# One semaphore per gather buffer, one-hots for two groups at a time, and one more hand-filled group each for ScalarE and VectorE, in a graph network layer

## The chip, the cores and the metric

One Trainium2 chip, one core. The metric is the device time of one execution in microseconds. The engines named below are PE (TensorE, matrix products; its weight loads are counted apart as PEld), DVE (VectorE), ACT (ScalarE), POOL (GpSimd, which here issues the indirect DMAs) and SP (SyncE, which issues the other DMAs). Each engine works through its own list of instructions in the order in which the program gives them, and engines wait for each other through semaphores.

## The reference

One message-passing layer over a graph of 12,500 nodes with 128 features and 400,000 edges, all in float32. The edges are sorted by their target node. Cut to what matters:

```python
h = jnp.maximum(_layernorm(x, axis=-1), 0.0)
e = jnp.concatenate([h[src], h[dst], edge_attr_32], axis=-1)      # 400000 x 288
m = jax.nn.relu(e @ w1 + b1) @ w2 + b2
agg = jax.ops.segment_sum(m, dst, num_segments=12500)
gi, gh = agg @ w_ih + b_ih, h @ w_hh + b_hh                       # GRU gates r, z, n
x + (1 - z) * n + z * h
```

## The kernel before

**Tiling.** 128 edges are a tile; 8 tiles are a group. The 3,125 tiles make 391 groups, numbered k from 0, of which the first has 5 tiles. A group is worked on in two halves, called units: unit u = 2k + h.

**What a group needs.** The product `e @ w1` is split in three. The part of the source node, `A = h @ w1[0:128]`, is computed once for all nodes in a first phase and written to DRAM. The part of the target node, `B`, too; since edges are sorted, a half group touches a window of at most 32 nodes, so its rows of B come as a block into `RW`, and a transposed one-hot `L` (made on DVE at L575) times `RW` adds them on PE into the PSUM tile `pre` (L673, which also does the edge attributes). The source rows are at random places, and there are four ways to get them:

- *Gathered*: POOL issues eight indirect DMAs (L156), one for each tile, that bring 128 rows of A into one of 11 buffers `G`. DVE then adds `pre` and `G` and takes the relu in one custom instruction (L701), which writes `RB`.
- *By hand on ACT*: ACT copies for each of the 1,024 edges one column of 4 bytes from `hT_all`, the transposed h that stays on the chip, into `HE_act` (L960). PE multiplies that with `w1a` into `pre` (L684), and ACT takes the relu (L710).
- *By hand on DVE*: the same with 512 instructions that pack two columns each into `both` (L967), and 8 copies that unpack them into `HE_dve` (L972).
- *By hand on SP*: 1,024 small DMAs from A into a buffer of their own.

For the addresses an engine that works by hand loads indices into its registers first: DVE 32 at a time (L945, 32 loads to a group), ACT 16 at a time.

The first 9 groups (`RAW`) gather rows of x instead of A, and are normalised on the way. `SPREAD` at L56 says how many of the other groups go by hand: 28 on ACT, 27 on DVE, 2 on SP, spread evenly over the list. That leaves 334 groups to POOL, 325 of them from A.

**Sum over edges.** A one-hot `OH` (128 edges by 32 nodes of the window for each tile, made on DVE at L623) is the weight of a product with `RB` on PE (L724), which collects two groups in one of two PSUM banks `seg`. The comparison row 0 to 31 of the one-hot stands in the unused part of the other bank. `take` copies the sums out (L733); every 14 groups a block of nodes goes through the gates (`node`).

**What sets the order.** The order of each engine's list is written out by hand (`manual_schedule`). The loop over units calls, for unit u: `gathers(u)`, then `stages(u)` with the transposed one-hot or the one-hot of group u//2 + 3, `pre(u+3)`, `add(u+2)` and `relu(u+2)`, then `seg(u)`; between them `run_jobs` puts the steps of the hand-filled groups in four portions. Each engine that fills by hand works on one group at a time, and its steps are spread over the units from the end of its last group to just before the group is needed. A gather may be put in the list once the DVE add that reads its buffer's old content stands before it.

**Semaphores.** The framework gives each indirect DMA one of eight semaphores (`DMASW0` to `DMASW7`) in turn. A DMA waits until the one eight before it, which used the same semaphore, has landed. The add of a group waits for all eight and for PE. An instruction has room for few waits; the others stand before it as EVENT_SEMAPHORE instructions of their own.

Of the kernel before, what the change touches and what calls it, by code (L numbers as in the profile page):

```python
# [9 lines left out]
F32 = mybir.dt.float32  # L10
# [19 lines left out]
V = 32  # L30
# [14 lines left out]
RAW = 9  # L45
GBUFS = 11
# [6 lines left out]
PIECE = 128  # L53
STEP = {"act": 4, "dve": 8, "sp": 4}
ROW = 4 * D
SPREAD = {"dve": 27, "act": 28, "sp": 2}  # L56
START = {"dve": 14, "act": 4, "sp": 24}
NR = 12672

# [4 lines left out]
def tile_gnn(ctx: ExitStack, tc: tile.TileContext, x, src, srcT, dstT, dstP, eaT, eaP, w1, b1, w2T, b2,  # L64
             wih, bih, whh, bhh, out):
    nc = tc.nc
    ctx.enter_context(tc.manual_schedule())
    const = ctx.enter_context(tc.tile_pool(name="const", bufs=1))
# [12 lines left out]
    def tiles(k):  # L81
        return (0 if k == 0 else SUP0 + (k - 1) * PAIR, SUP0 + k * PAIR)


    def unit_tiles(u):
        k, h = divmod(u, 2)
        t0, t1 = tiles(k)
        return [(t0 + a * GRP + j, j, a) for j in (2 * h, 2 * h + 1) for a in range(2)
                if t0 + a * GRP + j < t1]

    mode, order = {}, {m: [] for m in SPREAD}
    for m, n in SPREAD.items():
        lo, hi = START[m] // 2 + 2, NP - {"dve": 7, "act": 5, "sp": 12}[m]
        for i in range(n):
            k = lo + int((i + 1) * (hi - lo) / n)
# [46 lines left out]
    taker, ring = {}, []  # L142
    for k in range(NP):
        if k not in mode:
            taker[k] = ring[-GBUFS] if len(ring) >= GBUFS else -1
            ring.append(k)

    def gather(k):
        if k >= NP or k in mode:
            return  # L150
        G[k] = gp.tile([128, GRP, 2, D], F32, name="G")
        table = x if k < RAW else A
        for u in (2 * k, 2 * k + 1):
            for t, j, a in unit_tiles(u):
                c, i = divmod(t, CH)
                nc.gpsimd.indirect_dma_start(  # L156
                    out=G[k][:, j, a, :], out_offset=None, in_=table,
                    in_offset=bass.IndirectOffsetOnAxis(ap=src_i[c][:, i:i + 1], axis=0))

    for k in range(RAW):  # L160
        gather(k)
# [2 lines left out]
    RB = [const.tile([128, PAIR, D + 4], F32, name=f"RB{i}") for i in range(2)]  # L164
    for r in RB:
        nc.vector.memset(r[:, :, D:], 1.0)
    OHB = [const.tile([128, GRP, 2, V], F32, name=f"OH{i}") for i in range(6)]
    nc.vector.memset(OHB[0], 0.0)


# [93 lines left out]
    dloc = const.tile([128, T], F16, name="dloc")  # L264
# [78 lines left out]
    with tc.tile_pool(name="pp", bufs=3) as pp:  # L343
# [50 lines left out]
        row = lambda v: v.rearrange("(o f) -> o f", o=1)  # L394
# [34 lines left out]
        for q in range(NC + 3):  # L429
            if q < NC:  # L430
                b, i0, c, e, P, n0 = chunk(q)
# [3 lines left out]
            if 1 <= q <= NC:  # L435
                b, i0, c, e, P, n0 = chunk(q - 1)
# [6 lines left out]
            if q >= 3:  # L443
                b, i0, c, e, P, n0 = chunk(q - 3)
# [3 lines left out]
            if q < NC:  # L448
                b, i0, c, e, P, n0 = chunk(q)
# [4 lines left out]
            if 1 <= q <= NC:  # L454
                b, i0, c, e, P, n0 = chunk(q - 1)
# [12 lines left out]
            if q >= 3:  # L468
                b, i0, c, e, P, n0 = chunk(q - 3)
                if e == bats[b][1]:  # L470
                    nc.sync.dma_start(nodes(A, i0, e, P), asb[b][:P, :e, :])
            if 2 <= q <= NC + 1:
                b, i0, c, e, P, n0 = chunk(q - 2)
# [79 lines left out]
    Ls, OH, RT, HE, SEG = ({} for _ in range(5))  # L553
# [50 lines left out]
                                  "(p f) -> p f", p=V))  # L604

    def onehot(k):
        if k >= NP:
            return
        t0, t1 = tiles(k)
        OH[k] = OHB[k % len(OHB)]  # L610
        row = SEGB[((k - 3) // 2 + 1) % 2][:, 256:256 + V]
        for a in range(2) if k == 0 else (None,):
            if a is None:
                o, s = OH[k].rearrange("p j a v -> p a j v"), slice(t0, t1)
                d = dloc[:, s].rearrange("p (a j) -> p a j", a=2)[:, :, :, None]
                shape = [128, 2, GRP, V]
                i = row[:, None, None, :]
            else:
                e = min(t1, (a + 1) * GRP)
                o, d = OH[k][:, :e - a * GRP, a, :], dloc[:, a * GRP:e, None]  # L620
                shape = [128, e - a * GRP, V]
                i = row[:, None, :]
            nc.vector.tensor_tensor(o, d.to_broadcast(shape), i.to_broadcast(shape),  # L623
                                    op=ALU.is_equal)

    def unit(u):
        k, h = divmod(u, 2)
# [59 lines left out]
    def add(u):  # L687
        if u >= NU or u < 0:
            return
        k, h = divmod(u, 2)  # L690
        if h == 0 and k < NP - 1:
            return
        c = slice(0, PAIR) if k < NP - 1 else slice(GRP * h, GRP * h + GRP)
        o, p = RB[k % 2][:, c, :D], PP[k][:, c, :]
        if u in HE or k in hand:
            RT[u] = o, p
            HE.pop(u, None)
            HE.pop(u - 1, None)
            hand.pop(k, None)
        else:  # L700
            nc.vector._custom_dve(TENSOR_ADD_SAT, out=o, in0=p,  # L701
                                  in1=G[k].rearrange("p j a f -> p (j a) f")[:, c, :], s0=float("inf"), s1=0.0)
        if h == 1:
            PP.pop(k)
            G.pop(k, None)
# [9 lines left out]
    def seg(u):  # L715
        k, h = divmod(u, 2)
        p = SEGB[(k // 2) % 2]
        if h == 0 and k % 2 == 0:
            nc.tensor.matmul(p[:, :D + 1], zrow[:, :128], zrow[:, :D + 1], start=True, stop=False)  # L719
        l = unit_tiles(u)  # L720
        rest = l if h else l + unit_tiles(u + 1)
        for i, (t, j, a) in enumerate(l):
            r0 = 2 * V * (k % 2) + V * a
            nc.tensor.matmul(p[r0:r0 + V, :D + 1], OH[k][:, j, a, :],  # L724
                             RB[k % 2][:, 2 * j + a, :D + 1], start=False,
                             stop=all(b != a for _, _, b in rest[i + 1:]))

# [276 lines left out]
    def gathers(u):  # L1004
        while asked[0] < NP and (asked[0] in mode or 2 * taker[asked[0]] + 1 < u + 2):
            gather(asked[0])
            asked[0] += 1
# [13 lines left out]
    def stages(u):  # L1021
        if u + 7 >= 0:
            raw_stats(u + 7)
        if u + 6 >= 0:
            raw_fin(u + 6)
            raw_h(u + 6)
        if u % 2 == 0:
            onehot_T(u // 2 + 3)
        elif u > -7:
            onehot(u // 2 + 3)  # L1030
        if u + 4 >= 0:
            raw_turn(u + 4)
        if u + 3 >= 0:
            pre(u + 3)
        if u + 2 >= 0:
            add(u + 2)
            relu(u + 2)
# [18 lines left out]
    for u in range(NU):  # L1056
        k, h = divmod(u, 2)
# [33 lines left out]
        other(1)  # L1091
        other(2)
        seg(u)
        if u == 0:
            node_setup()
# [106 lines left out]
    f = nc.values_load(flag[0:1, 0:1], min_val=0, max_val=1)  # L1202
# [67 lines left out]
```

## Time and profile before

| what | value |
|---|---|
| time, median of 3 runs | 3404.46 us (3404.36 to 3407.26) |
| the profiled execution's own time | 3403.76 us |
| its span, first to last instruction | 3401.8 us |
| instructions | 88,642 |
| granted TensorE clock, mean | 0.796 |
| DMA | 335.44 MB, mean 99 GB/s |

The span is what the profile shows; 1.96 us of the profiled execution lie around it. Busy time counts an engine's own work; loads of registers, semaphore waits and branches are not in it, so an engine can be fully taken up with less than 100% busy. In a list of groups the last column gives the idle time just before the instructions and what ended it; "issue" means that the engine waited for nothing that the profile shows.

### The profile page before, as it was taken

To read this page: it belongs to the slowest core of one execution; us is meant where nothing else is said; L and a number is where in the kernel's file an instruction comes from. 1 tells how busy PE (TensorE), PEld (TensorE's weight loads), DVE (VectorE), ACT (ScalarE), POOL (GpSimd) and SP (SyncE) were. 2 spreads that over 40 slices of the span, in tenths; PEclk is the share of its full clock that TensorE was granted. 3 is DMA by queue.
4 is the path that set the end of the run, shared out by engine and by line. 5 is a ranking of instruction groups with operands and counts; after the bars stand their busy time and mean duration, and the time that the engine had idled before them with its cause. 6 is when DMAs were issued, how large, how long until landed. Compare 5 with 4: busy or idle time off the path is not lost. (4 is left out here: it accounts for less than half of the span.)

```text
span 3401.8 us, 88642 instructions
## 1 busy us (share of the span) xinstructions
PE 2417.4 (71%) x13113; PEld 1563.7 (46%) x13113; DVE 2225.1 (65%) x16468; ACT 3079.4 (91%) x29057; POOL 2566.1 (75%) x2678
## 2 busy tenths in 40 slices
PE   7567777777677767776777667676677767766767
PEld 7444444444445444544444444444444434444445
DVE  8556666666676666666666666666666666666665
ACT  7699999999999998999899988988988898898984
POOL 7777777777777777777777777777777777777776
PEclk9777887887887778777877877788777778777878
DMA  6434444434443333343434433443433334343332
GB/s 213 106 88 93 97 100 99 101 94 100 102 98 94 98 99 95 95 101 97 98 93 99 98 94 93 96 96 93 98 93 92 95 94 99 92 97 96 92 92 73
DMA packets 191316, 335.44 MB, mean 99 GB/s; under 512 B 66753, under 2 KB 112384, under 8 KB 190729
## 3 DMA queue, kind: packets, MB, share of 16 engines
q0 software_dynamic: 85408, 175.09, 23.0%
q1 hardware_dynamic: 105177, 154.58, 16.4%
q14 instruction: 478, 3.92, 0.4%
q8 instruction: 109, 1.79, 0.2%
q10 hardware_dynamic: 144, 0.07, 0.0%
HBM read 309.24 MB, written 20.24 MB: 97 GB/s over the span
## 5 line engine op out<-in xcount | busy, mean ns | idle before, releaser
L156 POOL DMA_INDIRECT G<-A,src_i x2600 | 2498.9, 961 | 796.2 <-issue 753.7
L960 ACT COPY HE_act<-hT_all 128x4 uint8 x28672 | 2886.8, 189 | 51.4 <-issue 27.0
L967 DVE SCALAR_TENSOR_TENSOR both<-hT_all 128x4 uint16 x13824 | 1173.4, 153 | 988.5 <-issue 980.7
L673 PE MATMUL pre<-RW,L 128*128 128x256 f32 x3128 | 1132.4, 488 | 229.8 <-DVE RB L701 220.6
L673 PEld LDWEIGHTS pre<-RW,L 128*128 128x128 f32 x3128 | 660.6, 236 | 506.1 <-DVE RB L701 234.0
L724 PE MATMUL seg<-RB,OH 128*32 128x129 f32 x6250 | 603.9, 324 | 380.0 <-DVE RB L701 349.7
L724 PEld LDWEIGHTS seg<-RB,OH 128*32 128x32 f32 x6250 | 333.1, 125 | 820.4 <-DVE RB L701 532.7
L701 DVE CUSTOM_DVE_ANT_0 RB<-pre,G 128x1024 f32<-128x1024 f32 (+1 forms) x326 | 394.5, 1210 | 62.7 <-DMA G<-A,src_i 49.2
L575 DVE TENSOR_SCALAR L<-L,node_of 64x512 f32<-64x512 int32 x382 | 186.7, 489 | 9.7 <-DMA L<-in_dstP 9.4
L719 PE MATMUL seg<-zrow 1*128 1x129 bf16 x196 | 45.3, 231 | 164.4 <-DVE OH L623 164.2
L623 DVE TENSOR_TENSOR OH<-dloc,seg 128x256 f32<-128x256 f16 (+1 forms) x392 | 159.5, 407 | 0.5 <-issue 0.5
L750 PE MATMUL nd<-spot,sums 128*128 128x40 f32 x782 | 116.6, 321 | 1.2 <-DVE sums L733 1.2
L750 PEld LDWEIGHTS nd<-spot,sums 128*128 128x128 f32 x782 | 112.4, 231 | 10.5 <-issue 9.0
L710 ACT ACTIVATE RB<-pre 128x1024 f32<-128x1024 f32 x64 | 65.0, 1015 | 52.4 <-PE pre L684 52.4
L809 ACT ACTIVATE gt<-nd 128x512 f32<-128x512 f32 (+2 forms) x28 | 16.4, 585 | 96.5 <-PE nd L803 96.5
L972 DVE COPY HE_dve<-both 128x512 uint8<-128x512 uint8 x216 | 96.6, 447 | 7.4
L684 PEld LDWEIGHTS pre<-w1a,HE_act 128*128 128x128 f32 x448 | 88.4, 245 | 11.6
L684 PEld LDWEIGHTS pre<-w1a,HE_dve 128*128 128x128 f32 x432 | 87.9, 252 | 12.1
L684 PE MATMUL pre<-w1a,HE_act 128*128 128x128 f32 x448 | 86.4, 327 | 0.0
L684 PE MATMUL pre<-w1a,HE_dve 128*128 128x128 f32 x432 | 85.1, 333 | 0.0
L156 POOL DMA_INDIRECT G<-in_x,src_i x69 | 65.9, 954 | 21.8 <-issue 20.7
L233 PE MATMUL nd<-w1b,hT_all 128*128 128x128 f32 x224 | 45.5, 346 | 43.3 <-DVE xb L835 43.3
(177 smaller groups left out, 1383.9 us busy)
## 6 DMA issues: line engine op xcount, KB each, us to landing
L<-in_dstP SPq DMA_DIRECT2D x195, 256.0 KB
L<-in_eaP SPq DMA_DIRECT2D x195, 256.0 KB
G<-A,src_i POOLq DMA_INDIRECT x2600
G_sp<-A SPq DMA_DIRECT2D x2048, 0.5 KB
RW<-B SPq DMA_DIRECT2D x782, 16.0 KB
xb<-in_x SPq DMA_DIRECT2D x26, 256.0 KB
out<-xb SPq DMA_DIRECT2D x26, 256.0 KB
xs<-in_x SPq DMA_DIRECT2D x11, 512.0 KB
```

The lines of the kernel that those rows point to most:

```text
L156: nc.gpsimd.indirect_dma_start(out=G[k][:, j, a, :], out_offset=None, in_=table, in_offset=bass.IndirectOffsetOnAxis(ap=src_i[c][:, i:i + ...
L575: nc.vector.tensor_scalar(o, i, node_of[:, k:k + 1], None, op0=ALU.is_equal)
L623: nc.vector.tensor_tensor(o, d.to_broadcast(shape), i.to_broadcast(shape), op=ALU.is_equal)
L673: nc.tensor.matmul(p[:, 2 * i:2 * i + 2, :], Ls[k // QP][:, c0:c0 + 128], RW[k % 4], start=True, stop=not raw)
L684: nc.tensor.matmul(p[:, 2 * i + a, :], cols, w1a, start=False, stop=n + 1 == len(l) or l[n + 1][1] != j)
L701: nc.vector._custom_dve(TENSOR_ADD_SAT, out=o, in0=p, in1=G[k].rearrange("p j a f -> p (j a) f")[:, c, :], s0=float("inf"), s1=0.0)
L710: nc.scalar.activation(o, p, AF.Relu)
L724: nc.tensor.matmul(p[r0:r0 + V, :D + 1], OH[k][:, j, a, :], RB[k % 2][:, 2 * j + a, :D + 1], start=False, stop=all(b != a for _, _, b in r ...
L750: nc.tensor.matmul(p[:, bass.ds(offs[i], V + SHIFT)], sums[:, slot(b, i), :D], spot[:, i % 2, :], start=False, stop=i == len(offs) - 1)
L960: nc.scalar.copy(he[:, e * 4:e * 4 + 4], column(v))
L967: nc.vector.scalar_tensor_tensor(both[:, (e0 % PIECE + i) // 2, :], column(vals[i + 1]), 256.0, column(vals[i]), op0=ALU.mult, op1=ALU.add)
L972: nc.vector.tensor_copy(he[:, p0 * 4:(p0 + PIECE) * 4].rearrange("p (n c b) -> p n c b", c=2, b=4), both.bitcast(U8).rearrange("p n (b c) ...
```

## The change

Three edits.

1. Each of the 11 buffers gets a semaphore of its own, `filled0` to `filled10`. The eight gathers of a group from A count it up by 16 each, and no longer use the framework's semaphores. Before the add DVE waits for this one semaphore to reach 128 times the number of uses of the buffer. The nine raw groups and the last group stay as they were.
2. The one-hots of two neighbouring groups are made by one instruction of twice the size. The six buffers of one group become three of two groups.
3. `SPREAD` goes to 29 groups on ACT and 28 on DVE. POOL keeps 332 groups, 323 of them from A.

```diff
-SPREAD = {"dve": 27, "act": 28, "sp": 2}
+SPREAD = {"dve": 28, "act": 29, "sp": 2}
...
+    filled = [tc.alloc_semaphore(f"filled{i}") for i in range(GBUFS)]
+    uses, goal = [0] * GBUFS, {}
+
     def gather(k):
         if k >= NP or k in mode:
             return
+        i = ring.index(k) % GBUFS
+        if RAW <= k < NP - 1:
+            uses[i] += 1
+            goal[k] = filled[i], 16 * PAIR * uses[i]
         G[k] = gp.tile([128, GRP, 2, D], F32, name="G")
...
-                nc.gpsimd.indirect_dma_start(
+                fetched = nc.gpsimd.indirect_dma_start(
                     out=G[k][:, j, a, :], out_offset=None, in_=table,
                     in_offset=bass.IndirectOffsetOnAxis(ap=src_i[c][:, i:i + 1], axis=0))
+                if k in goal:
+                    fetched.then_inc(goal[k][0], 16)
+                    tc.no_tile_sem_insts.add(fetched.ins.name)
+                    tc.add_to_no_dep_group(f"rows{k}", fetched.ins)
...
-    OHB = [const.tile([128, GRP, 2, V], F32, name=f"OH{i}") for i in range(6)]
+    OHB = [const.tile([128, 2 * PAIR, V], F32, name=f"OH{i}") for i in range(3)]
...
     def onehot(k):
-        if k >= NP:
+        if k >= NP or (k % 2 and k > 1):
             return
...
+        n = 2 if 1 < k < NP - 1 else 1
+        for i in range(n):
+            OH[k + i] = o[:, PAIR * ((k + i) % 2):PAIR * ((k + i) % 2) + PAIR, :]
+        t0, t1 = tiles(k)[0], tiles(k + n - 1)[1]
...
+        for p, e0, e1 in parts:
+            shape = [128, e1 - e0, V]
+            nc.vector.tensor_tensor(p, dloc[:, e0:e1, None].to_broadcast(shape),
+                                    row[:, None, :].to_broadcast(shape), op=ALU.is_equal)
...
         else:
-            nc.vector._custom_dve(TENSOR_ADD_SAT, out=o, in0=p,
+            if k in goal:
+                nc.vector.wait_ge(*goal[k])
+            made = nc.vector._custom_dve(TENSOR_ADD_SAT, out=o, in0=p,
                                   in1=G[k].rearrange("p j a f -> p (j a) f")[:, c, :], s0=float("inf"), s1=0.0)
+            if k in goal:
+                tc.declare_no_dep(made.ins, group=f"rows{k}", reason="behind the wait for the landing")
+                tc.declare_fence(made.ins, group=f"rows{k}")
...
-            nc.tensor.matmul(p[r0:r0 + V, :D + 1], OH[k][:, j, a, :],
+            nc.tensor.matmul(p[r0:r0 + V, :D + 1], OH[k][:, a * GRP + j, :],
                              RB[k % 2][:, 2 * j + a, :D + 1], start=False,
```

In the order of DVE's list, first two neighbouring groups before, from the one-hot ahead of the add of group 83 to the add of group 84. The ISA rows are the adds, `both` and `HE_dve` belong to a group that DVE fills by hand at that time, TENSOR_LOAD loads 32 indices, and the names in brackets are the semaphores that the instruction, or the EVENT_SEMAPHORE instructions just ahead of it, wait for:

```order
L623 TENSOR_TENSOR OH1_184<-dloc_227,seg0_79 128x2x4x32
L701 ISA RB1_180<-pre_39161,G_33482 128x8x128 [waits DMASW4_49,DMASW3_49,DMASW5_49,DMASW2_49,DMASW6_49,DMASW1_49,DMASW7_49,DMASW0_49,PE_49]
L967 SCALAR_TENSOR_TENSOR both_39049<-hT_all_60 128x4 x12
L972 COPY HE_dve_36483<-both_39049 128x512 [waits DVE_49]
L945 TENSOR_LOAD at_90
L967 SCALAR_TENSOR_TENSOR both_39877<-hT_all_60 128x4 x8
L575 TENSOR_SCALAR L_38458<-L_38458,node_of_230 64x512 [waits DMAHW4_49,DMAHW0_49]
L967 SCALAR_TENSOR_TENSOR both_39877<-hT_all_60 128x4 x8
L945 TENSOR_LOAD at_90
L967 SCALAR_TENSOR_TENSOR both_39877<-hT_all_60 128x4 x8
L623 TENSOR_TENSOR OH2_185<-dloc_227,seg0_79 128x2x4x32
L701 ISA RB0_179<-pre_39673,G_34018 128x8x128 [waits DMASW4_49,DMASW3_49,DMASW5_49,DMASW2_49,DMASW6_49,DMASW1_49,DMASW7_49,DMASW0_49,PE_49]
```

Each group has a one-hot of 256 elements in a row, and each add waits for nine semaphores. The same place in the changed kernel, from the add of group 93 to the add of group 94 (the lines have moved: 713 is the add, 633 the one-hot, 982, 987 and 960 the work by hand):

```order
L713 ISA RB1_180<-pre_45224,G_39434 128x8x128 [waits filled4,PE_49]
L960 TENSOR_LOAD at_90
L982 SCALAR_TENSOR_TENSOR both_45401<-hT_all_60 128x4 x16
L960 TENSOR_LOAD at_90
L982 SCALAR_TENSOR_TENSOR both_45401<-hT_all_60 128x4 x4
L586 TENSOR_SCALAR L_44384<-L_44384,node_of_227 64x512 [waits DMAHW4_49,DMAHW3_49]
L982 SCALAR_TENSOR_TENSOR both_45401<-hT_all_60 128x4 x12
L987 COPY HE_dve_42923<-both_45401 128x512 [waits DVE_49]
L960 TENSOR_LOAD at_90
L982 SCALAR_TENSOR_TENSOR both_46184<-hT_all_60 128x4 x8
L633 TENSOR_TENSOR OH0_183<-dloc_224,seg1_80 128x512
L713 ISA RB0_179<-pre_45680,G_39939 128x8x128 [waits filled5,PE_49]
```

Every second group makes the one-hots of two, and an add waits for two semaphores. DVE's list goes from 1,644 EVENT_SEMAPHORE instructions to 625, from 392 one-hots to 198, and gets one more group of 512 packing instructions, 32 register loads and 8 copies.

On POOL the gathers of group 42 before, and the first of the next group:

```order
L156 DMA G_14063<-A_97,src_i_1592 128x128 [waits DMASW5_49,DVE_49]
L156 DMA G_14063<-A_97,src_i_1592 128x128 [waits DMASW6_49]
L156 DMA G_14063<-A_97,src_i_1592 128x128 [waits DMASW7_49]
L156 DMA G_14063<-A_97,src_i_1592 128x128 [waits DMASW0_49]
L156 DMA G_14063<-A_97,src_i_1592 128x128 [waits DMASW1_49]
L156 DMA G_14063<-A_97,src_i_1592 128x128 [waits DMASW2_49]
L156 DMA G_14063<-A_97,src_i_1592 128x128 [waits DMASW3_49]
L156 DMA G_14063<-A_97,src_i_1592 128x128 [waits DMASW4_49]
L156 DMA G_14527<-A_97,src_i_1592 128x128 [waits DMASW5_49,DVE_49]
```

And those of group 42 in the changed kernel, with its neighbours on both sides:

```order
L163 DMA G_13796<-A_97,src_i_1590 128x128 [waits DVE_49]
L163 DMA G_13796<-A_97,src_i_1590 128x128 x7
L163 DMA G_14470<-A_97,src_i_1590 128x128 [waits DVE_49]
L163 DMA G_14470<-A_97,src_i_1590 128x128 x7
L163 DMA G_15456<-A_97,src_i_1590 128x128 [waits DVE_49]
L163 DMA G_15456<-A_97,src_i_1590 128x128 x7
```

What is left is one wait to a group, for the add that frees the buffer; the waits for the DMA eight places earlier are gone.

More of the change, by code (lines that the diff above doesn't have):

```diff
@@ L606, in onehot @@
     def onehot(k):
-        if k >= NP:
+        if k >= NP or (k % 2 and k > 1):
             return
-        t0, t1 = tiles(k)
-        OH[k] = OHB[k % len(OHB)]
+        o = OHB[(k // 2) % len(OHB)]
         row = SEGB[((k - 3) // 2 + 1) % 2][:, 256:256 + V]
[L612 to L624, printed above, removed]
+        n = 2 if 1 < k < NP - 1 else 1
+        for i in range(n):
+            OH[k + i] = o[:, PAIR * ((k + i) % 2):PAIR * ((k + i) % 2) + PAIR, :]
+        t0, t1 = tiles(k)[0], tiles(k + n - 1)[1]
+        if k:
+            parts = ((o[:, PAIR * (k % 2):PAIR * (k % 2) + t1 - t0, :], t0, t1),)
+        else:
+            parts = tuple((OH[0][:, a * GRP:min(t1, (a + 1) * GRP), :], a * GRP, min(t1, (a + 1) * GRP))
+                          for a in range(2))
+        for p, e0, e1 in parts:
+            shape = [128, e1 - e0, V]
+            nc.vector.tensor_tensor(p, dloc[:, e0:e1, None].to_broadcast(shape),
+                                    row[:, None, :].to_broadcast(shape), op=ALU.is_equal)
     def unit(u):
```

## The prediction

> **What bounds the kernel now.** I read the page's groups first, then the counts by stage of the instructions that touch `G`, then DVE's groups in the stretch from 400 to 1500 us. The page:
>
> ```profile
> PE 2417.4 (71%) x13113; PEld 1563.7 (46%) x13113; DVE 2225.1 (65%) x16468; ACT 3079.4 (91%) x29057; POOL 2566.1 (75%) x2678
> L156 POOL DMA_INDIRECT G<-A,src_i x2600 | 2498.9, 961 | 796.2 <-issue 753.7
> L960 ACT COPY HE_act<-hT_all 128x4 uint8 x28672 | 2886.8, 189 | 51.4 <-issue 27.0
> L967 DVE SCALAR_TENSOR_TENSOR both<-hT_all 128x4 uint16 x13824 | 1173.4, 153 | 988.5 <-issue 980.7
> ```
>
> By busy share ACT would be the bound. But POOL's idle time is all "issue": 753.7 us between 2,600 gathers, 0.3 us ahead of each. Busy and idle together are 2498.9 + 796.2 = 3295 us, the whole run but its first 92 us. The line's own view and two pieces of POOL's timeline show that it never stops:
>
> ```profile
> L156 POOL DMA_INDIRECT G<-A,src_i x2600: 940/945/1552, 92.3 to 3383.9; - x186
> 5.92 0.94 POOL L156 DMA_INDIRECT G<-in_x,src_i  x1 [0.30 <-issue]
> 203.40 0.95 POOL L156 DMA_INDIRECT G<-A,src_i  x1 [0.72 <-DVE RB L701]
> ```
>
> From the first to the last start are (3383.9 - 92.3) / 2599 = 1.2665 us a gather. The gather at 5.92 us, the third of the run, has no wait for an earlier DMA and still a gap of 0.30 us, so the gap is not a wait for semaphores.
>
> Does POOL set the end, or does it only happen to be busy until then? Counts by stage (POOL: gathers, DVE: adds):
>
> ```profile
> core 0: us, PE busy (x) PEld busy (x) DVE busy (x) ACT busy (x) POOL busy (x), PEclk, DMA share, GB/s
> 0.00:202.00 202.00, 14.07 (x69) 9.00 (x69) 14.93 (x70) 28.41 (x69) 149.06 (x157) 0.85 0.51 148
> 202.00:400.00 198.00, 0.00 (x0) 0.00 (x0) 25.39 (x21) 0.00 (x0) 149.84 (x157) 0.77 0.40 94
> 400.00:1000.00 600.00, 0.00 (x0) 0.00 (x0) 77.61 (x64) 0.00 (x0) 454.88 (x473) 0.82 0.41 99
> 1000.00:1500.00 500.00, 0.00 (x0) 0.00 (x0) 62.79 (x52) 0.00 (x0) 379.60 (x396) 0.79 0.39 96
> 1500.00:1700.00 200.00, 0.00 (x0) 0.00 (x0) 25.51 (x22) 0.00 (x0) 152.14 (x158) 0.82 0.40 98
> ```
>
> At 202 us POOL has begun 157 gathers, 20 groups (the first has five), and the work on them has only got through the nine raw ones, with DVE at its first add: all 11 buffers are full. At 1700 us it is 1,341 gathers, 168 groups, against 9 + 21 + 64 + 52 + 22 = 168 (an instruction across an edge counts twice). So the rest of the kernel starts 11 groups late, catches up until 1700 us, and from there waits for POOL:
>
> ```profile
> 400.00:1500.00 1100.00, 140.40 (x116) 0.81 0.40 98
> 400.00:1500.00 1100.00, 20.32 (x20) 0.81 0.40 98
> 1700.00:2800.00 1100.00, 131.35 (x109) 0.78 0.39 95
> 1700.00:2800.00 1100.00, 19.32 (x19) 0.78 0.39 95
> ```
>
> These are, for two stretches of 1100 us, the busy time (with the number) first of the adds (L701), then of the relus of hand-filled groups (L710): 136 groups at 8.09 us each while it catches up, 128 at 8.59 once it depends on POOL. The last add starts 1.7 us after the last gather ends, and the rest of the tail is fixed:
>
> ```profile
> 3383.95 0.94 POOL L156 DMA_INDIRECT G<-A,src_i  x1 [0.30 <-issue]
> 3386.64 0.69 DVE L701 CUSTOM_DVE_ANT_0 RB<-pre,G 128x512 f32<-128x512 f32 x1 [3.67 <-DMA G<-A,src_i]
> ```
>
> What sets 8.09 us? DVE, as its groups in that stretch and the row of all engines show:
>
> ```profile
> 400.00:1500.00 1100.00, 800.11 (x4348) 508.44 (x4346) 747.88 (x5693) 1049.83 (x10240) 834.47 (x868) 0.81 0.40 98
> L967 DVE SCALAR_TENSOR_TENSOR both<-hT_all 128x4 uint16 x5008 | 424.9, 153 | 339.8 <-issue 333.8 <-DMA G_sp<-A 5.2
> L701 DVE CUSTOM_DVE_ANT_0 RB<-pre,G 128x1024 f32<-128x1024 f32 x116 | 140.7, 1213 | 3.9 <-PE pre L673 2.9 <-DMA G<-A,src_i 0.5 <-issue 0.4
> L623 DVE TENSOR_TENSOR OH<-dloc,seg 128x256 f32<-128x256 f16 x136 | 55.5, 408 | 0.0
> L972 DVE COPY HE_dve<-both 128x512 uint8<-128x512 uint8 x78 | 34.9, 447 | 2.7
> ```
>
> DVE is busy for 747.9 us and idle for 333.8 us at the packing (its register loads); 18 us are left of 1100. ACT, with 1049.8 us, is next.
>
> **The change part by part.** The sum is made on the profiled span of 3401.8 us.
>
> *POOL loses 16 gathers*: 16 x 1.2665 = -20.3 us, on the path, as long as DVE and ACT keep up.
>
> *POOL loses its waits*: 0, by the gap of 0.30 us at 5.92 us. A gain is excluded by that row; I see no loss.
>
> *DVE gets a hand-filled group.* The stretch has 5008 / 512 = 9.78 of them, which cost 424.9 + 333.8 + 34.9 = 793.6 us, 81.1 us each. Two groups leave the add: -2 x 1.2. Together +78.7.
>
> *One-hots*: 194 instructions fewer. From 256 elements in 408 ns and the add's 1024 in 1213 ns an element takes 1.05 ns and the fixed part is 140 ns, which gives 676 ns for 512 (estimate) and saves 140 ns a pair. But neighbours overlap:
>
> ```profile
> 1005.42 0.41 DVE L623 TENSOR_TENSOR OH<-dloc,seg 128x256 f32<-128x256 f16 x1
> 1005.75 1.21 DVE L701 CUSTOM_DVE_ANT_0 RB<-pre,G 128x1024 f32<-128x1024 f32 x1
> ```
>
> From start to start it is 0.33 us, 268 ns of it elements, so 62 ns. The saving lies between 194 x 62 and 194 x 140 ns, 12 to 27 us; I take 18.
>
> *Semaphores on DVE*: three EVENT_SEMAPHOREs fewer at each of some 322 adds.
>
> ```profile
> L701 DVEq EVENT_SEMAPHORE  x1358: 21/50/2846, 201.2 to 3386.5; - x194
> L945 DVEq TENSOR_LOAD <-at x864: 2095/2150/3239, 188.2 to 3336.5; - x173
> ```
>
> They take 50 ns of DVE's issue, beside running work. They cost time only where issue is late, and it is late at the register loads (TENSOR_LOAD): 2.15 us each, of which 333.8 us / (9.78 x 32) = 1.07 us stay uncovered. A semaphore ahead of a load moves it back. Bounds: 0, and 966 x 50 ns = 48 us; I take 25, since some adds have no load close behind.
>
> The Trainium skill speaks against this term: "VectorE: DVE Perf Modes", section "Rules for kernel authors", says to cut the number of operations, "not sems". By it the term is 0, and the end that is worked out below for DVE is 25 us later, still hidden. The trace's 50 ns rows neither bear it out nor refute it, since they don't say what lies uncovered; it enters the chance of the first rival below.
>
> DVE together: +78.7 - 18 - 25 = +36 us, between +3 and +67. DVE starts group 9's add at 201.9 us:
>
> ```profile
> 201.92 1.21 DVE L701 CUSTOM_DVE_ANT_0 RB<-pre,G 128x1024 f32<-128x1024 f32 x1
> ```
>
> At 8.09 us the 381 groups after it would now end at 3284 us, 103 us ahead of the actual 3386.6. With +36 they end at 3320, with +67 at 3351; POOL would give the last add at 3386.6 - 20.3 = 3366.3. So POOL remains the bound, with the cover down from 103 us to 46 (15 to 82).
>
> *ACT gets a hand-filled group*: 2886.8 / 28 = 103 us and two relus of 1 us. 1049.8 / 136 = 7.72 us a group makes 381 x 7.72 + 105 = 3046 and an end at 3248: hidden behind POOL, with 118 us of cover.
>
> *Contention*: a gather has a median of 945 ns and a mean of 961. If DVE's work by hand is all of that, 16 ns x 2600 / 27 = 1.5 us for one group more; bounds 0 and 1.5, taken 0.5. The Trainium skill, "SBUF — State Buffer", section "Who interferes with whom", says that a copy on VectorE can lock GpSimd out for its whole length. By that eight copies of 447 ns cost up to 3.6 us, and the sum below would be -15.7; the longest gather, 1552 ns, agrees with such a lock.
>
> *The start*: while all buffers are full, each us that DVE is late stops POOL. It did so for 0.72 - 0.30 = 0.42 us at 203.40. From 202 to 400 us the queue of full buffers falls only from 11 to 9.6, and hand-filled groups now come at 17, 22, 30, 35 instead of 17, 22, 31, 36. Below nothing: -0.4, if DVE's relief comes first. Above: one group's time, +8. I take +1.
>
> Sum: -20.3 + 0.5 + 1.0 = -18.8; span 3383.0, profiled execution 3385.0. The median shown is 0.7 us above the profiled execution: 3385.7 us.
>
> **The rivals.**
>
> *DVE, ACT and PE together become the bound (the other side).* This decides above (3366.3 - 201.9) / 381 = 8.305 us a group. DVE at its upper bound (+67, no gain from semaphores) needs 8.27. If half of the time that ACT spent waiting for PE and DVE there now comes back on DVE, since ACT has less lead, that is 17 of 34 us for 136 groups, 0.13 more:
>
> ```profile
> L710 ACT ACTIVATE RB<-pre 128x1024 f32<-128x1024 f32 x20 | 20.3, 1016 | 14.8 <-PE pre L684 14.8
> L809 ACT ACTIVATE gt<-nd 128x512 f32<-128x512 f32 x9 | 5.3, 591 | 15.7 <-PE nd L803 15.7
> ```
>
> (The other 3.9 us are L819's.) At 8.39 the last add starts at 3398.5, 12 us later than before: 3416 us. For it: 98% of DVE's time in that stretch is accounted for. Against: it takes the upper bound twice.
>
> *POOL starves at the start.* Eight us lost while the buffers are full, nothing regained: 3393 us. For it: the full queue at 202 us. Against: one wait of 0.42 us in 2,600.
>
> *The gathers themselves get faster* without their eight semaphores, by 10 ns: 26 us more, 3360 us. Against it stands the gap at 5.92 us.
>
> **How the numbers follow.** The forecast, POOL as the bound and 3382 to 3390 us: 0.62. Starving, 3390 to 3397: 0.11. The rival loop: 0.24, from 3392 upward, of which 0.04 faster, 0.07 the same, 0.13 slower. Faster gathers: 0.03. A measurement of this kernel can tell about 0.2% (6.8 us) from no change; that gives faster 0.80, same 0.07, slower 0.13. The range is 3381 to 3400 us: below it are the faster gathers, above it most of the rival loop.
>
> **What would show it.** Right: 2,584 gathers from A at 1.266 us, the last start near 3364 us, and still no gaps but "issue"; an add 2 to 4 us behind it; 133 to 138 groups between 400 and 1500 us; DVE's add waiting for landings after 1700 us or somewhat later; one-hots of 128x512 near 676 ns. Wrong: waits of POOL for L713 well past 400 us; adds that never come to wait for landings; a last add more than 10 us behind the last gather; or gathers whose mean leaves 955 to 965 ns.

## The result and the profile after

| kernel | median us | lowest to highest | runs | profiled execution | its span |
|---|---|---|---|---|---|
| before | 3405.09 | 3402.62 to 3407.54 | 20 | 3403.76 | 3401.8 |
| the change | 3409.24 | 3402.18 to 3414.34 | 20 | 3404.30 | 3402.5 |

The ratio is 1.0011 (95% interval 1.0004 to 1.0018), 4 us more and within 0.2% of no change. The prediction had 3385.7 us, 24 us below what was measured. The change also spreads more, 12 us against 5, and its profiled execution is 5 us below its median, so its trace shows a good run.

The page of the change, its totals and five groups (line, engine, operation, output and input, count; then busy us and mean ns; then idle us before it and what ended it), and behind them the add's group on the page of before:

```profile
PE 2416.6 (71%) x13145; PEld 1554.1 (46%) x13145; DVE 2252.0 (66%) x16792; ACT 3184.5 (94%) x30083; POOL 2553.4 (75%) x2662
L163 POOL DMA_INDIRECT G<-A,src_i x2584 | 2486.3, 962 | 791.5 <-issue 768.6
L982 DVE SCALAR_TENSOR_TENSOR both<-hT_all 128x4 uint16 x14336 | 1214.0, 156 | 1005.8 <-issue 997.9
L713 DVE CUSTOM_DVE_ANT_0 RB<-pre,G 128x1024 f32<-128x1024 f32 x324 | 393.0, 1213 | 25.4 <-PE pre L683 24.5
L633 DVE TENSOR_TENSOR OH<-dloc,seg 128x512 f32<-128x512 f16 (+1 forms) x198 | 132.7, 671 | 0.0
```

```profile
L701 DVE CUSTOM_DVE_ANT_0 RB<-pre,G 128x1024 f32<-128x1024 f32 (+1 forms) x326 | 394.5, 1210 | 62.7 <-DMA G<-A,src_i 49.2
```

The gathers did what was forecast: 16 fewer, 962 ns each (961 before), and a one-hot for two groups takes 671 ns. But the add no longer waits for landings. Of its 62.7 us of idle time before, 49.2 ended with a transfer; what is left now ends with PE. POOL has stopped being the bound. The line's own view of the gathers (shortest, median and longest ns; first and last start), and the end of POOL's and DVE's timelines (start, length):

```profile
L163 POOL DMA_INDIRECT G<-A,src_i x2584: 940/944/1546, 91.9 to 3366.6; - x199
```

```profile
3366.56 0.94 POOL L163 DMA_INDIRECT G<-A,src_i  x1 [0.30 <-issue]
...
3382.75 1.29 DVE L713 CUSTOM_DVE_ANT_0 RB<-pre,G 128x512 f32<-128x512 f32 x2 [3.00 <-PE pre L683]
```

The last gather ends at 3367.5 us, 17.4 us sooner than before. The last add starts 15 us behind it instead of 1.7: the 17 us that POOL gave are lost in front of the add. Counts by stage of the change: all engines in two stretches of 1100 us, then the adds (L713), then the relus of hand-filled groups (L725):

```profile
core 0: us, PE busy (x) PEld busy (x) DVE busy (x) ACT busy (x) POOL busy (x), PEclk, DMA share, GB/s
400.00:1500.00 1100.00, 790.02 (x4303) 499.95 (x4303) 740.92 (x5661) 1062.50 (x10359) 835.74 (x867) 0.80 0.40 97
1700.00:2800.00 1100.00, 768.78 (x4192) 482.42 (x4194) 728.89 (x5573) 1056.85 (x10186) 835.08 (x869) 0.79 0.40 96
...
400.00:1500.00 1100.00, 137.56 (x113) 0.80 0.40 97
1700.00:2800.00 1100.00, 134.99 (x111) 0.79 0.40 96
...
400.00:1500.00 1100.00, 20.25 (x20) 0.80 0.40 97
1700.00:2800.00 1100.00, 19.79 (x20) 0.79 0.40 96
```

These are 133 groups and then 131. The prediction needed 8.305 us a group or less to stay with the gathers; over the whole run the change has (3382.8 - 201.3) / 381 = 8.35 (its add of group 9 starts at 201.3 us). By the interpolated paces of the table below it is at that limit in the first stretch (8.294) and too slow in the second (8.453).

### The profile page after: what moved, and what is told of

Its sections match the earlier page's. It is cut to its first block, busy times and chain, and to the rows that moved or that the text cites. A ratio compares the mean times of both kernels' runs of the same rounds, so it can differ in the third digit from the quotient of the medians.

```text
span 3402.5 us, 88725 instructions
## 1 busy us (share of the span) xinstructions
PE 2416.6 (71%) x13145; PEld 1554.1 (46%) x13145; DVE 2252.0 (66%) x16792; ACT 3184.5 (94%) x30083; POOL 2553.4 (75%) x2662
## 5 line engine op out<-in xcount | busy, mean ns | idle before, releaser
L975 ACT COPY HE_act<-hT_all 128x4 uint8 x29696 | 2993.5, 189 | 56.1 <-issue 30.6
L982 DVE SCALAR_TENSOR_TENSOR both<-hT_all 128x4 uint16 x14336 | 1214.0, 156 | 1005.8 <-issue 997.9
L713 DVE CUSTOM_DVE_ANT_0 RB<-pre,G 128x1024 f32<-128x1024 f32 x324 | 393.0, 1213 | 25.4 <-PE pre L683 24.5
L633 DVE TENSOR_TENSOR OH<-dloc,seg 128x512 f32<-128x512 f16 (+1 forms) x198 | 132.7, 671 | 0.0
L848 PE MATMUL nd<-ident,gt 128*128 128x128 f32 (+2 forms) x112 | 27.5, 388 | 92.5 <-DVE gt L844 90.5
L725 ACT ACTIVATE RB<-pre 128x1024 f32<-128x1024 f32 x66 | 66.8, 1012 | 15.4 <-PE pre L694 15.4
```

The source lines that it names most:

```text
L633: nc.vector.tensor_tensor(p, dloc[:, e0:e1, None].to_broadcast(shape), row[:, None, :].to_broadcast(shape), op=ALU.is_equal)
L713: made = nc.vector._custom_dve(TENSOR_ADD_SAT, out=o, in0=p, in1=G[k].rearrange("p j a f -> p (j a) f")[:, c, :], s0=float("inf"), s1=0.0)
L725: nc.scalar.activation(o, p, AF.Relu)
L975: nc.scalar.copy(he[:, e * 4:e * 4 + 4], column(v))
L982: nc.vector.scalar_tensor_tensor(both[:, (e0 % PIECE + i) // 2, :], column(vals[i + 1]), 256.0, column(vals[i]), op0=ALU.mult, op1=ALU.add)
```

## The experiments

Three theories. **D**: DVE's own time (its instructions and the part of its register loads that nothing covers) sets the pace. **A**: ACT sets it, alone or through PE. **S**: the new semaphores cost time themselves. "Spread" is the number of hand-filled groups of DVE, ACT and SP. All kernels below are the changed one with the edit shown. Eight runs fell on one chip, on which the kernel before took 3402.84 (first four) and 3402.88 us (second four). Ten fell on two other chips, on which it took 5656 to 5716 us. The change itself was timed apart from all of them, beside the kernel before at 3405.09 us, so kernels of different occasions are best compared by their ratios.

**e1_edits12**, without edit 3 (spread 27, 28, 2):

```diff
-SPREAD = {"dve": 28, "act": 29, "sp": 2}
+SPREAD = {"dve": 27, "act": 28, "sp": 2}
```

> Edits 1 and 2 alone: SPREAD stays at 28 on ACT and 27 on DVE. Theory D (DVE's own time, instructions plus uncovered register loads, sets the pace of the loop in the changed kernel, and one hand-filled group more on it is what overdid it): POOL is the bound again, 2600 gathers from A with the last start near 3384 us, DVE catches up by 1700 us or earlier and waits for landings after that; 3401 to 3406 us. Theory A (ACT, alone or through PE, sets the pace): the same 3401 to 3406, as ACT has its 28 groups again. Theory S (the new semaphores themselves cost time, in landings or in the add's wait): 3409 us or more, slower than before by as much as the change is.

Measured 3407.38 us, ratio 1.0017 (1.0008 to 1.0026).

**e2_spread**, edit 3 alone: the kernel before with

```diff
-SPREAD = {"dve": 27, "act": 28, "sp": 2}
+SPREAD = {"dve": 28, "act": 29, "sp": 2}
```

> Edit 3 alone: 29 and 28 groups by hand, with the old eight semaphores and a one-hot for each group. Theory D with edits 1 and 2 worth what the prediction took (18 + 25 us of DVE): the loop is DVE-bound and DVE has 43 us more to do than in the changed kernel, so 3445 to 3455 us. Theory D with edits 1 and 2 worth next to nothing: 3409 to 3418 us, within 10 us of the changed kernel. Theory A: edits 1 and 2 only touch DVE, so 3405 to 3412 us like the changed kernel. Theory S: faster than the changed kernel, 3385 to 3395 us.

Measured 3461.14 us, ratio 1.0181 (1.0167 to 1.0195).

**e3_act29**, ACT's added group without DVE's:

```diff
-SPREAD = {"dve": 28, "act": 29, "sp": 2}
+SPREAD = {"dve": 27, "act": 29, "sp": 2}
```

> The changed kernel with DVE back at 27 groups, ACT at 29: 8 gathers fewer than before. Theory D: the loop's pace is back near 8.1 us a group and POOL is the bound, 8 x 1.2665 = 10 us less than before: 3393 to 3398 us. Theory A: ACT has the same 29 groups as in the changed kernel and is the bound: 3405 to 3412 us. Theory S: 3405 us or more.

Measured 3397.53 us, ratio 0.9982 (0.9974 to 0.9991): the best of all, and the only one whose interval lies below 1 on that chip.

**e4_dve28**, DVE's added group without ACT's:

```diff
-SPREAD = {"dve": 28, "act": 29, "sp": 2}
+SPREAD = {"dve": 28, "act": 28, "sp": 2}
```

> The changed kernel with ACT back at 28 groups, DVE at 28: 8 gathers fewer than before. Theory D: DVE has the same work as in the changed kernel and its pace holds: 3405 to 3412 us. Theory A: 3393 to 3398 us, POOL the bound. Theory S: 3405 us or more.

Measured 3405.71 us, ratio 1.0013 (1.0004 to 1.0022).

What follows: D, but not from every run. e1_edits12 alone doesn't tell: it lies 1.4 us above D's range, and its ratio of 1.0017 beside the change's 1.0011 is what S forecast. S falls with e2_spread, which is slower without the new semaphores, and with e3_act29, which is faster than before with them. e2_spread came 6 us above the highest range that was written down for it, so edits 1 and 2 were worth more than any theory had. D rests on the last two: with 27 groups on DVE the loop falls back to the gathers whether ACT has 28 or 29, with 28 it doesn't. The add's groups of e3_act29 and of e4_dve28 show it, the first waiting for transfers, the second for PE:

```profile
L713 DVE CUSTOM_DVE_ANT_0 RB<-pre,G 128x1024 f32<-128x1024 f32 (+1 forms) x325 | 394.0, 1212 | 76.1 <-DMA G<-A,src_i 64.1
```

```profile
L713 DVE CUSTOM_DVE_ANT_0 RB<-pre,G 128x1024 f32<-128x1024 f32 x324 | 392.5, 1212 | 23.5 <-PE pre L683 22.6
```

And edits 1 and 2, worth nothing to the time of e1_edits12, are worth 52 us (3461.1 - 3409.2; 58 us by the ratios) once DVE decides.

**e5_rows** deals out the rows of `at` anew. It came from a look at the loads: in every trace until then DVE's load takes 2.20 us for the first list or two, 2.10 to 2.12 us up to 1640 to 1780 us and 2.15 us or more after that, and the list of a later group lies in a higher partition, so that hour and place can't be told apart.

```diff
-    by_hand = [k for m in ("sp", "act", "dve") for k in order[m]]
+    by_hand = order["sp"] + order["dve"][:12] + order["act"][:18] + order["dve"][12:] + order["act"][18:]
```

> The changed kernel with only the rows of `at` dealt out anew: VectorE's 28 lists of nodes lie in partitions 2-13 and 32-47, ScalarE's in 14-31 and 48-58 (in the change VectorE has 31-58). In every trace so far VectorE's 32-value load takes 2.20 us from partitions 30 and 31, 2.10 from 32 to 39, 2.12 from 40 to 43, 2.15 to 2.17 from 44 on, which can be the place or the hour. Theory P (the place sets it): loads of 2.10 us at partitions 2-7 and 32-39, 2.12 at 8-11 and 40-43, 2.15 at 12-13 and 44-47, a mean of 2.116 against 2.136, 896 loads, so 18 us less of VectorE's time; with D (VectorE's own time sets the loop) the last add comes 13 to 17 us sooner, close behind the last gather: 3392 to 3397 us. Rival (the loads grow with the hour): the loads step up near 1650 us as before, and 3409 +- 3 us. Rival A (ScalarE sets the loop): its loads grow by some 0.013 us in the mean, 1856 of them, 24 us if nothing hides them: 3409 to 3430 us.

Measured 5744.99 us, where before took 5706.57 (ratio 1.0063, 1.0040 to 1.0086): an answer for another loop than the first chip's. It ran again as **e9_rows**:

> e5_rows again, on another chip: there the kernel before took 5707 us, ScalarE's copies waited 2055 us for issue (27 us in the profile of before) and the adds stayed 170 us behind the gathers throughout, so its time says nothing of this loop. Its rows already show that VectorE's load goes with the place of its list: 2.10 us at partitions 32 to 39 between 2600 and 3960 us, 2.15 at 44 to 47. Theory P with D: where the kernel before takes 3400 to 3408 us, this one has 18 us less of VectorE's time and its last add close behind the last gather: 3392 to 3397 us. Rival A (ScalarE, whose loads grow by 24 us in all): 3409 to 3430 us. Rival (loads are covered by other work): 3406 to 3412 us.

Measured 3399.83 us, ratio 0.9996 (0.9987 to 1.0004). DVE's loads from 1650 to 2800 us (lowest, median, highest ns; first and last start) of the change and of e9_rows, and those of e9_rows behind 2958 us, which come from partitions 44 to 47:

```profile
L960 DVEq TENSOR_LOAD <-at x324: 2131/2154/3159, 1649.9 to 2798.2; - x162
```

```profile
L960 DVEq TENSOR_LOAD <-at x327: 2095/2105/3046, 1651.1 to 2798.5; - x164
...
L960 DVEq TENSOR_LOAD <-at x104: 2133/2151/3017, 2958.2 to 3323.2; - x104
```

The place sets the duration, not the hour. The gain is 5 us by the ratios, 9 by the medians, where 12 to 17 were expected: right in kind, half in size.

**e6_pairs** has edits 2 and 3 with the old semaphores (short of all that edit 1 brings):

```diff
-            if k in goal:
-                nc.vector.wait_ge(*goal[k])
-            made = nc.vector._custom_dve(TENSOR_ADD_SAT, out=o, in0=p,
+            nc.vector._custom_dve(TENSOR_ADD_SAT, out=o, in0=p,
```

> Paired one-hots and the spread 28/29, with the old semaphores. Edits 1 and 2 together were worth 52 us in the bound loop (3461.1 without them, 3409.2 with them on other runs). The prediction's split of 25 to 18 for semaphores and one-hots makes 30 of the 52 the semaphores': 3436 to 3444 us here. Rival (semaphores cost nothing, only operations do): 3405 to 3413 us. Rival (they are all of it): 3455 to 3465 us.

**e7_sems** has edits 1 and 3 with the old one-hots (the edit is cut to its start):

```diff
-        if k >= NP or (k % 2 and k > 1):
+        if k >= NP:
             return
-        o = OHB[(k // 2) % len(OHB)]
+        t0, t1 = tiles(k)
+        OH[k] = OHB[k % len(OHB)]
```

> The new semaphores and the spread 28/29, with the old one-hots of one group each. By the prediction's split the one-hots are 22 of the 52 us: 3427 to 3435 us. Rival (only the number of operations costs): 3455 to 3465 us. Rival (semaphores are all of it): 3405 to 3413 us. The two halves of e6_pairs and this one should add up to the 52 us, if each acts by itself.

**e8_act30** puts the added group on ACT:

```diff
-SPREAD = {"dve": 28, "act": 29, "sp": 2}
+SPREAD = {"dve": 27, "act": 30, "sp": 2}
```

> The change with VectorE 27, ScalarE 30, SyncE 2: as many gathers as the change (2,584 from A), the added group on ScalarE. D (VectorE's own time sets the loop's pace): VectorE has one group fewer (81 us), so it falls back to the gathers; the last gather ends near 3364 to 3368 us, the add within 4 us of it: 3384 to 3391 us. A (ScalarE sets it): ScalarE has 30 groups of 103 us and no more slack than 20 us in 1100: the adds stay 15 us or more behind the last gather, 3403 us or more.

Measured with before at 5706.57: 5747.76 (1.0061, 1.0043 to 1.0080), 5724.81 (1.0025, 1.0007 to 1.0042) and 5919.50 us (1.0369, 1.0343 to 1.0395). They too ran again.

> e6_pairs again, where the kernel before takes 3400 to 3408 us. As before: the prediction's split 3436 to 3444 us; semaphores cost nothing 3405 to 3413 us; they are all of the 52 us 3455 to 3465 us.

**e10_pairs**: 3468.85 us, ratio 1.0188 (1.0175 to 1.0202).

> e7_sems again, where the kernel before takes 3400 to 3408 us. As before: the prediction's split 3427 to 3435 us; only the number of operations costs 3455 to 3465 us; semaphores are all of it 3405 to 3413 us.

**e11_sems**: 3411.03 us, ratio 1.0023 (1.0014 to 1.0032). So "all of it" held for the semaphores (e10_pairs came 4 us above that range). They bring 1.58% beside the old one-hots (1.0181 to 1.0023, 54 us) and 1.77% beside the new (1.0188 to 1.0011, 60 us). The paired one-hots bring -0.12% with the new semaphores and +0.07% with the old: nothing that can be measured. Both forecasts by the prediction's split fell.

> e8_act30 again, where the kernel before takes 3400 to 3408 us. As before: D 3384 to 3391 us; A 3403 us or more. On the chip where ScalarE's copies waited for issue it was the slowest by 3.7%, as A says for a loop that ScalarE does set; here ScalarE has 33 us to spare in 1100.

**e12_act30**: 3453.65 us, ratio 1.0153 (1.0140 to 1.0166). D's 3384 to 3391 fell, A's side held. The row of all engines of e12_act30:

```profile
400.00:1500.00 1100.00, 787.50 (x4246) 495.29 (x4246) 719.08 (x5429) 1084.25 (x10589) 835.18 (x869) 0.80 0.39 96
```

ACT is busy for 1084 of 1100 us: with 30 groups it is the bound itself. In the change, with 29, it is at 1062.5 and DVE decides. But beside 27 groups on DVE ACT is the bound of the loop with 29 as well, as the same row of e3_act29 shows (1086 of 1100 us); there its 8.10 us a group are still fast enough for the gathers:

```profile
400.00:1500.00 1100.00, 808.51 (x4372) 509.22 (x4371) 742.02 (x5614) 1085.71 (x10605) 835.35 (x869) 0.80 0.40 98
```

**e13_dve29**, **e14_low** and **e15_sp3** were to settle the price of a group on DVE, the place of the lists, and a third group on SP:

```diff
-SPREAD = {"dve": 28, "act": 29, "sp": 2}
+SPREAD = {"dve": 29, "act": 28, "sp": 2}
```

> The change with VectorE 29, ScalarE 28, SyncE 2; beside e4_dve28 (28/28, 3405.7 us, last add 3385 us in its trace) one hand-filled group more on VectorE alone. The prediction priced such a group by its mean share: 81 us, with 1.07 us of each of its 32 loads uncovered. By that 3475 to 3490 us. Theory M (the added loads have no cover of their own, and thin out that of the others: from the kernel before to e2_spread the early stretch went from 8.09 to 8.39 us a group, 115 us in 381): 3505 to 3530 us.

```diff
-    by_hand = [k for m in ("sp", "act", "dve") for k in order[m]]
+    by_hand = [k for m in ("sp", "dve", "act") for k in order[m]]
...
+    low = [r + p for b in (0, 8) for r in (0, 32, 64, 96) for p in range(b, b + 8) if r + p not in (64, 96)]
+    at_p = dict(zip(by_hand, low))
...
-        r = by_hand.index(k)
+        r = at_p[k]
```

> The change with the lists of nodes in the low rows of all four quarters of the partitions: VectorE's 28 in 2-7, 32-39, 65-71 and 97-103, ScalarE's behind them in each quarter (8-15, 40-47, 72-79, 104-108), and three more instructions to place them. P: VectorE's loads 2.10 us and ScalarE's 1.02 to 1.03 us in the whole run, if each quarter is like the others. With D the early pace of 8.29 us a group then holds to the end: the last add near 201.9 + 381 x 8.29 = 3360 us, so the gathers decide (last one near 3366): 3385 to 3392 us. Rival (the pace falls late for another reason, or ScalarE decides): 3398 to 3409 us.

```diff
-SPREAD = {"dve": 28, "act": 29, "sp": 2}
+SPREAD = {"dve": 27, "act": 29, "sp": 3}
```

> VectorE 27, ScalarE 29, SyncE 3: as many gathers as the change, the added group filled by SyncE's transfers of one row each. D: VectorE and ScalarE as in e3_act29, which fell back to the gathers, and 10 us less of gathers: 3384 to 3391 us. Rival (SyncE's queue gets too long: its 1,024 transfers come late, or hold back the loads of L and RW): 3400 us or more, with PE waiting for SyncE's transfers.

Measured 5614.46 (0.9829, 0.9804 to 0.9854), 5729.44 (1.0029, 1.0013 to 1.0046) and 5833.52 us (1.0212, 1.0186 to 1.0237), with before at 5716.47: again such a chip. The second try fell on one as well:

> e14_low again, where the kernel before takes 3400 to 3408 us (it took 5716 there, with ScalarE's copies waiting for issue as in the runs of e5 to e8). Its rows show loads of 2.10 us on VectorE and 1.02 to 1.03 us on ScalarE throughout. As before: 3385 to 3392 us by D and P; 3398 to 3409 us if the pace falls late for another reason or ScalarE decides.

> e13_dve29 again, where the kernel before takes 3400 to 3408 us. As before: 3475 to 3490 us by the mean share of a hand-filled group (81 us), 3505 to 3530 us by theory M (115 us or more).

> e15_sp3 again, where the kernel before takes 3400 to 3408 us. As before: 3384 to 3391 us if SyncE's transfers hold nobody back (in e15_sp3 the adds of SyncE's three groups waited 3 us in all); 3400 us or more if its queue delays the loads of L and RW.

Measured 5697.06 (1.0076, 1.0049 to 1.0104), 5585.43 (0.9877, 0.9846 to 0.9908) and 5799.35 us (1.0255, 1.0222 to 1.0288), with before at 5656.33. ACT's copies in e16_low by its page, and by their line its loads and DVE's:

```profile
L981 ACT COPY HE_act<-hT_all 128x4 uint8 x29696 | 3243.7, 189 | 2064.9 <-issue 2036.8
```

```profile
L966 ACTq TENSOR_LOAD <-at x1856: 1019/1026/2027, 227.8 to 5644.0; - x186
L966 DVEq TENSOR_LOAD <-at x896: 2096/2102/3006, 300.0 to 5626.0; - x180
```

A copy takes 189 ns as ever, but ACT waits 2037 us for issue, and there ACT decides: DVE 29 with ACT 28 is 1.2 to 1.7% faster than before, DVE 27 with ACT 30 3.7% slower. For the loop of the first chip these ten times say nothing, and the forecasts of e13_dve29 to e18_sp3 stay untested. They do show that loads from the low rows of all four quarters of the partitions take 2.10 and 1.03 us to the end of a run of 5.7 ms.

## Why the prediction was wrong, point by point

The pace of each kernel, from the starts of the adds and relus, interpolated at the ends of the stretch, and the uncovered part of a load, which is the "issue" time of DVE's packing group from 400 to 1500 us over its loads (one for 16 instructions):

| kernel | DVE, ACT | semaphores, one-hots | us a group, 400 to 1300 | 400 to 1500 | 1700 to 2800 | uncovered, us a load |
|---|---|---|---|---|---|---|
| before | 27, 28 | old, old | 8.080 | 8.090 | waits for POOL | 1.066 |
| e1_edits12 | 27, 28 | new, new | 7.952 | 8.035 | waits for POOL | 1.015 |
| e3_act29 | 27, 29 | new, new | 8.130 | 8.096 | waits for POOL | 1.019 |
| e12_act30 | 27, 30 | new, new | 8.363 | 8.387 | 8.546 | 1.037 |
| e2_spread | 28, 29 | old, old | 8.414 | 8.391 | 8.567 | 1.127 |
| e10_pairs | 28, 29 | old, new | 8.490 | 8.429 | 8.668 | 1.140 |
| e11_sems | 28, 29 | new, old | 8.351 | 8.299 | 8.448 | 1.063 |
| e4_dve28 | 28, 28 | new, new | 8.412 | 8.386 | 8.348 | 1.098 |
| the change | 28, 29 | new, new | 8.327 | 8.294 | 8.453 | 1.079 |
| e9_rows | 28, 29 | new, new | 8.313 | 8.293 | 8.333 | 1.092 |

The column to 1300 us stands there because of e1_edits12. Its loop is so fast that it has caught up with the gathers early: its add waits for landings from 1354 us on, 10.5 us up to 1500 us, so that its 8.035 is in part POOL's pace:

```profile
L713 DVE CUSTOM_DVE_ANT_0 RB<-pre,G 128x1024 f32<-128x1024 f32 x117 | 142.2, 1216 | 11.4 <-DMA G<-A,src_i 10.5 <-PE pre L683 0.5
```

The last column of the table for e1_edits12, e2_spread and the change comes from these rows, one of each kernel's groups from 400 to 1500 us:

```profile
L982 DVE SCALAR_TENSOR_TENSOR both<-hT_all 128x4 uint16 x5043 | 426.9, 154 | 328.1 <-issue 319.8 <-DMA G_sp<-A 7.1
```

```profile
L967 DVE SCALAR_TENSOR_TENSOR both<-hT_all 128x4 uint16 x4993 | 422.7, 154 | 354.0 <-issue 351.6 <-DMA L<-in_dstP 1.8
```

```profile
L982 DVE SCALAR_TENSOR_TENSOR both<-hT_all 128x4 uint16 x5056 | 427.4, 156 | 344.1 <-issue 340.9 <-DMA RW<-B 2.3
```

A pace is good to some 0.1 us, 38 us in 381 groups: e4_dve28 has less work than the change and came out 0.09 slower early, with some 14 us of waits for PE on DVE in that stretch, and 0.1 faster late, with none.

- *POOL loses 16 gathers*: right. The last gather started at 3366.6 us, forecast "near 3364"; 962 ns, within 955 to 965.
- *POOL's waits, contention*: right in kind. No gain, and a gather's mean went from 961 to 962 ns, some 3 us in all where 0.5 stood.
- *The start*: forecast +1. POOL waited 1.33 us at 122.9 us, 0.40 at 284.8 and 1.03 at 327.0, 1.9 us beyond its gap of 0.30, where it had been 0.42: right within a us. The first place is one that the prediction didn't look at; the kernels of the first chip wait there for 0.8 to 2.5 us, with old and new semaphores alike.
- *One-hots*: forecast 18 us. The instruction's price was right (676 forecast, 671 measured), its worth was not: nothing measurable. That the saving is in busy time, while the loop hangs on issue, is the likely reason; no run tests it.
- *Semaphores*: forecast 25 us, between 0 and 48. Measured 54 to 60, above the bound, since the count was too small as well: at the add there are 58 of 50 ns and 276 of 21 ns now, against 1,358 of 50 ns. That is 1358 x 50 - 58 x 50 - 276 x 21 = 59 us, as if every one of them counted in full. The last adds of the profiled executions, single ones, put it at 39 us (e2_spread to e11_sems) and 64 us (e10_pairs to the change).

```profile
L713 DVEq EVENT_SEMAPHORE  x58: 21/50/50, 201.0 to 3382.8; - x58
...
L712 DVEq EVENT_SEMAPHORE  x276: 21/21/21, 217.1 to 3369.2; - x138
```

The Trainium skill, "VectorE: DVE Perf Modes", section "Rules for kernel authors", says of chained DVE operations to keep their count low, "not sems". Carried over to this loop, 198 one-hots in place of 392 should pay and the semaphores not. These runs decide the other way, for waits that are instructions of their own in a loop held by issue: 54 to 60 us for the semaphores, nothing measurable for the one-hots.

- *DVE gets a hand-filled group, +81 us*: **this is the step that failed first.** It took 1.07 us uncovered for each of the 32 added loads and left the other loads as they were. But with 28 groups instead of 27 the mean load is covered less: 1.127 against 1.066 us with the old edits, 1.079 and 1.098 against 1.015 and 1.019 with the new, whatever ACT has. 0.06 us of 896 loads is 54 us. The pace from 400 to 1500 us puts the whole at (8.391 - 8.090) x 381 = 115 us instead of 79. Counted to 1300 us, before e1_edits12 waits for landings, the pairs of the table with one DVE group between them give 127 us (before to e2_spread), 143 (e1_edits12 to the change) and 175 (e1_edits12 to e4_dve28, which differ in DVE's group alone). Only e3_act29 to the change gives 75, and there ACT already holds the pace of e3_act29. All this points to more than the 81 us at which the group was priced; how much more the paces don't tell well, and the run that was to tell fell on the other chips. Whether the added loads themselves find no cover or thin out that of the others stays open.
- *8.09 us for all 381 groups*: **the second step that failed.** The stretch from 400 to 1500 us stood for the whole run. Behind 1640 us DVE's loads come from higher partitions and take 2.15 instead of 2.10 us, 0.05 x 32 x 28 / 376 = 0.12 us a group. Before, this lay behind the gathers and didn't show. e9_rows gave back about that, 8.453 to 8.333 at the same 8.29 early, and an uncovered part of 1.073 us a load late (337.5 us for 5031 / 16 loads) where the change has 1.136 (353.4 us for 4978 / 16). This step is at the limit of what a pace tells, and e4_dve28, with loads of 2.15 us late and still 8.348, doesn't show it.
- *The sum*: DVE's edits together were to cost +36 us and end at 3320, 46 ahead of POOL. Edit 3 alone was to end at 3284 + 79 = 3363, and e2_spread's last add is at 3430: 67 late, of which the early pace makes 36 (201.9 + 381 x 8.391 = 3399) and what follows 31. Edits 1 and 2 then took 47 in the traces, 43 forecast. So the sum missed by 63 us, all of it in edit 3 and in the pace that it was added to, while two wrong sizes in edits 1 and 2 nearly cancelled.
- *ACT gets a hand-filled group*: hidden behind POOL, as forecast (e3_act29 has the best time of all), but by less than the 118 us named. The loop itself did get slower by it, from 7.952 to 8.130 us a group (e1_edits12 to e3_act29 up to 1300 us), 68 us in 381 groups: there ACT was already the bound. Its next group, in e12_act30, 8.363, was then too slow for the gathers.
- *The rivals*: the first is the one that came, the loop as the bound beyond 8.305 us a group. It forecast 8.39 and 3416 us; 8.35 and 3409 came. Its mechanism, ACT's waits coming back on DVE, isn't what the traces show: from 400 to 1500 us ACT's waits for PE and DVE fell from 34 to 20 us, but DVE's waits for PE and ACT stayed at 7.0 and 8.7 us. And with 28 groups on DVE, ACT's added group makes no difference beyond the 0.1 us (e4_dve28, 8.412, against the change, 8.327). POOL didn't starve, and the gathers didn't get faster.

Left open: e1_edits12 is 4.5 us slower than before though it only removes work. Its last gather ends 1.8 us later, behind a wait of 2.15 us at 124.2 us, and 2.1 us more lie behind its last add; neither was traced to a cause. Also open is whether lists in low rows, or a third group on SP, would make as many gathers as the change has pay on a chip like the first.

## What to carry to other kernels

A pace measured in one stretch, before the bottleneck moves, is only the pace of that stretch: ask what changes later in the run and is hidden there today, and look whether the loop doesn't wait for another bound within the stretch already. Where an engine's gaps are "issue", its price list is another one. Here about half of each register load showed (1.02 to 1.14 of 2.1 us), the semaphore waits counted about in full, the instructions saved counted for nothing measurable, and one job more was dearer than the mean of those that were there. Before moving work onto a second engine that is 95% busy, do it to one engine at a time: ACT's group alone gained 0.18%, and DVE's beside it lost that again.

## What the hardware showed unasked

- A register load takes as long as the place of its source says. DVE's, of 32 values: 2.20 us from partitions 30 and 31, 2.10 from 32 to 39, 2.12 from 40 to 43, 2.15 to 2.17 from 44 to 58, and 2.10 again from 65 to 71 and 97 to 103. ACT's, of 16 values, go from 1.02 us at partition 2 to 1.06 at 28. The first 32 loads of the change come from partition 31, the first 64 of before from 30 and 31, and both have a median of 2.205 us; e9_rows moved the steps with the rows.
- On two chips other than the first the kernel before takes 5656 to 5716 us instead of 3403. In the kernels profiled there instructions and loads are as long as elsewhere (copies of 189 to 190 ns on ACT), but ACT's copies wait 2010 to 2153 us for issue with 28 or 29 groups, 25 to 31 us elsewhere: stretches of up to some 200 copies without a gap change with stretches in which every one to three copies come 0.4 to 1.3 us late. What holds the issue back there wasn't settled.
